# A list-scheduling planner that orders by due time instead of by rank, and six more tiles of exponents turned through DRAM, in a fused attention and state-space kernel

## The chip, the cores and the metric

The kernel runs on one core of a Trainium2 chip. The metric is the device time of one execution in microseconds, as the median of three runs. All arithmetic is float32, but for the mask and some idle matmuls.

## What is computed

The input is `X` of 4 batches x 1024 tokens x 256 features. Four residual layers follow one another, each on a layernorm of the running `x` (cut from the reference, with the names that the kernel uses in front):

```python
# a: causal attention
scores = where(causal, -inf, Q @ K.T / 16);  x = x + softmax(scores) @ V
# f: a feed-forward that mixes each token with the one before it
xr, xk = mu * xn + (1 - mu) * xn_prev
x = x + sigmoid(xr @ W_r.T) * (relu(xk @ W_k.T) ** 2 @ W_v.T)
# h, s: a state-space layer: projections, a causal convolution over the whole
#       sequence with 16 decay kernels, a skip and a gate silu(z)
x = x + (((conv(xp @ W_B.T) @ W_C.T + D_skip * xp) * silu(z)) @ W_out.T + b_out)
# g: the feed-forward once more, with the same weights
```

## The kernel before

**Tiles.** The whole `x` stays on chip. The tokens are cut into 32 tiles `i` of 128 (batch `i // 8`, place in the batch `t = i % 8`) and into 8 halves `j` of 512 (four tiles). Attention works by tiles: `scores(i)` (L1075) multiplies the queries of a tile with the `t + 1` blocks of keys before it; VectorE takes out the row extreme while it copies them to SBUF (`least`, L1098), ScalarE takes the exponents (`exponents`, L1108), the exponents are turned so that keys lie on partitions, and `weigh(i)` (L1181) multiplies them with the values (`po` on TensorE). The other layers work by halves.

**Two ways to turn.** `turn(i)` (L1158) has TensorE transpose each 128x128 block into PSUM (`ppt`), and ScalarE or VectorE copies it out. `turn_by_dram(i)` (L1124) has SyncE write the exponents to DRAM (L1135, `exps<-pr`), read them back in four pieces in another order (L1141, `pblocks<-exps`), and VectorE transposes 32x32 blocks (L1146, `prT<-pblocks`). Before the change the tiles with `t` of 0 and 1 of every batch take the first way and those with `t` of 2 to 7 the second (`TURNED_BY_DRAM = 2`, L38, used at L1100, L1490 and L1496). The normalized halves of layers a, f, h and g are turned through DRAM as well (`by_dram`, L482: one write of 512 KB at L489, four reads at L495, two transposes at L501), except four at the seams.

**The planner.** The order in which instructions stand on each engine is not written by hand but worked out when the kernel is built, by the class `Order` (L48). TensorE's work is a list of *units* in a fixed order, the order in which the main loop (L1486) and the lines behind it call them. All else is *ops*: a key, the keys it needs, one or more engines with a cost in us, and a lag until the result can be used. A unit first lets the planner place every op that can start by then (L121), and then takes TensorE for its own cost. Among the ops on offer the one with the earliest start goes first; of those with the same start (the engine is busy and several are waiting) the one with the lowest `rank`, then the one that was ready first (L94 to L96). Ranks: 0 for most; 1 for the normalizations of a, f and h on VectorE (L385); 2 for `by_dram`'s DMAs; 3 for loads, stores and the decay table (L247, L691, L806, L1339). Each engine then runs its list strictly in order, SyncE's DMA queue too, and waits in place for what an instruction needs.

**Hand-set holds.** `normalized` (L374) has a parameter `after`. With it the 512 KB write of a normalized half waits in the plan until the reads of a given tile of exponents have been issued and their lag has passed (`behind`, L995; given at L1010, L1221 and L1517).

**Loads.** `load` (L243) puts a planned time `at` on a list of transfers. Only the last transfer of a list carries the key that others need (L247). One list is `mu` (L311, at 14.0): two transfers for `muk` and then two for `mur`. The op `mu1` (L367) has VectorE work out `1 - mu` from all four (`complements`, L364).

The loop that calls the units of attention:

```python
for i in range(-2, NI):
    first, second = mix_units(i)
    if i + 2 < NI:
        scores(i + 2)
        if (i + 2) % NT >= TURNED_BY_DRAM:
            turn_by_dram(i + 2)
    for unit in first:
        unit()
    if 0 <= i + 1 < NI and (i + 1) % NT < TURNED_BY_DRAM:
        turn(i + 1)
```

## Time and profile before

| what | us |
|---|---|
| median of three runs (475.33 to 476.75) | 475.8 |
| the profiled execution | 476.57 |
| its span, first to last instruction | 474.8 |
| TensorE busy, share of the span | 99% |
| VectorE, ScalarE, GpSimd busy | 67%, 40%, 23% |
| DMA engines busy, mean of 16 | 50% |

The profile is of one execution. Its engines are PE (TensorE matmul), PEld (its weight load), DVE (VectorE), ACT (ScalarE), POOL (GpSimd) and SPq (the DMA queue of SyncE). `L1189` is a line of the kernel. A line of the timeline gives the start, the time from the first start to the last end of a run of like instructions, the engine, the line, the operation, what it writes and reads, and in brackets how long the engine was idle before it and what ended that. A matmul's recorded duration overlaps the next one's, so what a matmul costs is read from start to start.

### The profile page before, as it was taken

Reading aid. Unit: us, or ns where it says so; the run is one execution under the profiler, and the core shown is the slowest. Engines: PE = TensorE matmul, PEld = TensorE weight load, DVE = VectorE, ACT = ScalarE, POOL = GpSimd, SP = SyncE. Lnnn points to the kernel's source line nnn. Section 1 sums busy time; section 2 is a strip of 40 time slices with the busy share of each in tenths; the row PEclk is TensorE's granted clock in tenths of the full one; section 3 lists DMA queues with packets and bytes.
Section 4 is the critical chain, followed back from the end, with each engine's and each line's share of the span. In section 5 each row is a group of like instructions: output and inputs, shape, how many; then the busy total and the mean of one; then the engine's idle time right before and its main releaser. Section 6 shows DMA issues by size and latency. Waiting matters only on the chain.

```text
span 474.8 us, 6474 instructions
## 1 busy us (share of the span) xinstructions
PE 468.3 (99%) x2114; PEld 320.4 (67%) x2114; DVE 319.2 (67%) x856; ACT 190.2 (40%) x346; POOL 110.6 (23%) x119
## 2 busy tenths in 40 slices
PE   8999999999999999999999999999999999999996
PEld 5766676765866766866758766465565774877765
DVE  4657677698798797794986875410669794986312
ACT  3431435343346244344354385501113643535332
POOL 3020103101603304422223245300002210233330
PEclk9999999999999999999999999999999999999999
DMA  7649677634833944817249494902122706126112
GB/s 205 200 106 270 198 182 169 182 100 129 253 65 106 278 133 133 242 32 218 69 143 284 162 253 123 330 4 63 50 89 76 212 22 177 46 72 195 45 66 66
DMA packets 78289, 68.24 MB, mean 144 GB/s; under 512 B 13536, under 2 KB 75952, under 8 KB 78256
## 3 DMA queue, kind: packets, MB, share of 16 engines
q1 hardware_dynamic: 77440, 67.57, 48.9%
q8 instruction: 16, 0.26, 0.2%
q10 hardware_dynamic: 816, 0.26, 0.2%
q14 instruction: 17, 0.14, 0.1%
HBM read 39.95 MB, written 27.86 MB: 143 GB/s over the span
## 4 chain that ended last, share of the span: by engine, by line
PE 78%; DVE 10%; DMA 6%; SPq 3%; issue 2%; POOL 0%; ACT 0%; DVEq 0%; ACTq 0%
PE po L1189 8%; PE sc L1089 8%; PE py L1394 6%; PE pv L1061 3%; DMA pblocks<-exps 2%; DMA exps<-pr 2%; SPq L1141 2%; PE pc L1347 2%; DMA blocks_f<-rows_f 1%; PE dust L899 1%; DVE pr L1104 1%; DVE prT L1146 1%; PE py L1406 1%; SPq L495 1%; DVE hT_f L501 1%
## 5 line engine op out<-in xcount | busy, mean ns | idle before, releaser
L1189 PE MATMUL po<-v,prT 128*128 128x256 f32 x288 | 67.9, 380 | 0.5 <-DVE prT L1146 0.5
L1089 PE MATMUL sc<-xa,q 128*128 128x512 f32 (+3 forms) x192 | 67.2, 486 | 0.0
L1189 PEld LDWEIGHTS po<-v,prT 128*128 128x128 f32 x288 | 54.1, 189 | 11.0 <-issue 2.1
L1109 ACT ACTIVATE pr<-pr,nmx 128x128 f32<-128x128 f32 (+7 forms) x32 | 24.8, 774 | 71.9 <-DVE pr L1104 66.5
L1089 PEld LDWEIGHTS sc<-xa,q 128*128 128x128 f32 x192 | 35.1, 190 | 23.4 <-issue 18.9
L1061 PE MATMUL pv<-wv,xa 128*128 128x257 f32 x128 | 33.5, 384 | 0.0
L680 POOL TENSOR_TENSOR x<-x,r_f 128x512 f32<-128x512 f32 x16 | 22.5, 1410 | 40.0 <-DVE r_f L674 40.0
L427 POOL TENSOR_TENSOR rs_h<-ve_h,minus_half 128x8 f32<-128x8 f32 x8 | 13.2, 1646 | 78.1 <-DVE ve_f L414 38.9
L1104 DVE TENSOR_SCALAR_CACHE_REDUCE pr<-sc,v 128x128 f32<-128x128 f32 (+7 forms) x32 | 25.6, 799 | 7.0 <-PE sc L1096 6.8
L1146 DVE STREAM_TRANSPOSE prT<-pblocks 128x384 f32<-128x384 f32 (+5 forms) x24 | 21.7, 905 | 10.7 <-DMA pblocks<-exps 10.7
L1394 PE MATMUL py<-xnT,wk 128*128 128x512 f32 x64 | 28.8, 595 | 0.0
L1061 PEld LDWEIGHTS pv<-wv,xa 128*128 128x128 f32 x128 | 23.2, 191 | 8.0 <-issue 4.8
L680 POOL TENSOR_TENSOR x<-x,r_g 128x512 f32<-128x512 f32 x14 | 18.9, 1355 | 35.2 <-DVE r_g L674 34.2
L1234 POOL TENSOR_TENSOR x<-x,bout_r 128x512 f32<-128x512 f32 x16 | 20.2, 1274 | 26.8 <-ACT x L1227 17.7
L427 POOL TENSOR_TENSOR rs_g<-ve_g,minus_half 128x4 f32<-128x4 f32 x8 | 8.4, 1045 | 74.5 <-DVE ve_g L414 74.5
L1416 DVE SCALAR_TENSOR_TENSOR z<-py,b_skip,z 128x512 f32<-128x512 f32 x16 | 10.9, 743 | 21.6 <-PE py L1406 21.6
L1199 DVE SCALAR_TENSOR_TENSOR x<-po,rsm,x 128x256 f32<-128x256 f32 x32 | 15.5, 483 | 14.3 <-PE po L1189 11.2
L1394 PEld LDWEIGHTS py<-xnT,wk 128*128 128x128 f32 x64 | 12.0, 190 | 13.7 <-issue 13.5
L595 ACT ACTIVATE xk_g<-hT_g,muk 128x512 f32<-128x512 f32 x16 | 10.6, 712 | 20.3 <-DVE hT_g L501 20.3
L595 ACT ACTIVATE xk_f<-hT_f,muk 128x512 f32<-128x512 f32 x16 | 10.7, 714 | 19.7 <-DVE hT_f L501 11.8
L1227 ACT ACTIVATE x<-x,mrs_h,rs 128x256 f32<-128x256 f32 x32 | 17.5, 588 | 0.0
L1071 DVE TENSOR_TENSOR v<-pv,bv_r 128x257 f32<-128x257 f32 x32 | 13.2, 412 | 4.4 <-PE pv L1061 4.0
(431 smaller groups left out, 948.7 us busy)
## 6 DMA issues: line engine op xcount, KB each, us to landing
hk<-r_dram SPq DMA_DIRECT2D x16, 512.0 KB, 8.9
rows_g<-xn_g SPq DMA_DIRECT2D x8, 512.0 KB
blocks_g<-rows_g SPq DMA_DIRECT2D x32, 128.0 KB, 2.7
x<-in_L_attn_a_X_dram SPq DMA_DIRECT2D x7, 512.0 KB, 4.3
rows_f<-xn_f SPq DMA_DIRECT2D x7, 512.0 KB
blocks_f<-rows_f SPq DMA_DIRECT2D x28, 128.0 KB, 2.7
rows_h<-xn_h SPq DMA_DIRECT2D x7, 512.0 KB, 4.4
blocks_h<-rows_h SPq DMA_DIRECT2D x28, 128.0 KB, 3.0
```

Of the source, the lines that this page charges most:

```text
L427: nc.gpsimd.tensor_tensor(rs()[:, :k].rearrange("p k n -> p (k n)"), ve()[:, :k].rearrange("p k n -> p (k n)"), minus_half[:, : k * NH], A ...
L595: nc.scalar.mul(t()[:, c, :], hT()[:, c, 1:], mu[:, c : c + 1])
L680: nc.gpsimd.tensor_add(xg, xg, r()[:, ts(g, 2), :])
L1061: nc.tensor.matmul(pv()[:, : D + 1], lhsT=xaj()[:, c, ts(n, P)], rhs=wv[:, c, :], start=(c == 0), stop=(c == KC - 1),)
L1089: nc.tensor.matmul(sc()[:, k * HALF : k * HALF + w], lhsT=qh()[:, c, ts(n, P)], rhs=keys[k]()[:, c, :w], start=(c == 0), stop=(c == KC - 1 ...
L1104: nc.vector.tensor_scalar(dst, src, vh()[:, n, D : D + 1], None, ALU.add, ALU.min, accum_out=nmx(),)
L1109: nc.scalar.activation(p()[:, :nk], p()[:, :nk], AF.Exp, bias=nmx(), scale=-1.0, accum_out=sm())
L1146: nc.vector.transpose(dst()[:, : NH * width].rearrange("p (k m a) -> p k m a", m=NH, a=GRP), blocks().rearrange("p m (k a) -> p k m a", a= ...
L1189: nc.tensor.matmul(po()[:, :D], lhsT=src()[:, ts(n, P)], rhs=v[2 * b + n // NH]()[:, n % NH, :D], start=(n == 0), stop=(n == t),)
L1227: nc.scalar.activation(xt, xt, AF.Identity, bias=mrs()[:, 0, n : n + 1], scale=rs1()[:, n : n + 1])
L1234: nc.gpsimd.tensor_add(xg, xg, bout_r.unsqueeze(1).to_broadcast([P, 2, D]))
L1394: nc.tensor.matmul(dst()[:, ts(e, HALF)], lhsT=w_x[:, c, ts(e, P)], rhs=src()[:, c, :], start=(c == 0), stop=False,)
```

## The change

The class `Order` first writes everything into a log, and places it only in `finish`. In between it works out a due time for each entry, backwards. Ranks and `after` are gone; `behind` is deleted. `TURNED_BY_DRAM` keeps its value of 2 and is now compared with the tile's number instead of its place in the batch, so that only tiles 0 and 1 are turned by TensorE, and tiles 8, 9, 16, 17, 24 and 25 go through DRAM. What `op`, `unit` and `_step` did with the engines' times stays as it was.

```diff
+    def op(self, key, needs, *ways, frees=None, delay=0.0, lag=LAG):
+        self.log.append(dict(
+            kind="op", key=key, needs=needs, ways=ways, frees=frees, delay=delay, lag=lag,
+            cost=min(c for _, c, _ in ways),
+        ))
...
+    def _due(self):
+        log = self.log
+        made = {e["key"]: n for n, e in enumerate(log) if e["key"] is not None}
+        due = [math.inf] * len(log)
+        at = 0.0
+        takes = {kind: [] for kind in self.BANKS}
+        for n, e in enumerate(log):
+            if e["kind"] == "unit":
+                due[n] = at
+                at += e["cost"]
+            if e.get("takes"):
+                takes[e["takes"]].append(at)
+        given = {kind: 0 for kind in self.BANKS}
+        for n, e in enumerate(log):
+            if e["kind"] == "op" and e["frees"]:
+                kind = e["frees"]
+                k = given[kind] + self.BANKS[kind]
+                given[kind] += 1
+                if k < len(takes[kind]):
+                    due[n] = takes[kind][k] - self.LAG - e["cost"]
+        order = self._sorted(made)
+        for n in reversed(order):
+            e = log[n]
+            for k in e["needs"]:
+                m = made[k]
+                if log[m]["kind"] in ("op", "unit"):
+                    d = due[n] - e.get("delay", 0.0) - log[m]["lag"] - log[m]["cost"]
+                    due[m] = min(due[m], d)
+        return due
...
     def _first(self):
-        start, _, _, n = min(
-            (self._way(op)[1], op["rank"], op["time"], n) for n, op in enumerate(self.offered)
+        start, _, _, k = min(
+            (self._way(time, n)[1], self.due[n], time, k)
+            for k, (time, n) in enumerate(self.offered)
         )
...
-            o.op(key if last else None, [f"t{at}", *after], (queue, 0.5, emit), lag=lag, rank=3)
+            o.op(key if last else None, [f"t{at}", *after], (queue, 0.5, emit), lag=lag)
...
-            by_dram(key, xn, parts + list(after), dst, names)
+            by_dram(key, xn, parts, dst, names)
...
-    def behind(i):
-        if not 0 <= i < NB * NT:
-            return []
-        return [f"e{i}.r{P // GRP - 1}" if i % NT >= TURNED_BY_DRAM else f"e{i}"]
...
-            if t >= TURNED_BY_DRAM:
+            if i >= TURNED_BY_DRAM:
...
-            if (i + 2) % NT >= TURNED_BY_DRAM:
+            if i + 2 >= TURNED_BY_DRAM:
                 turn_by_dram(i + 2)
...
-        if 0 <= i + 1 < NI and (i + 1) % NT < TURNED_BY_DRAM:
+        if 0 <= i + 1 < TURNED_BY_DRAM:
             turn(i + 1)
...
-                mix1.prepare(i // NH, by_hand=i == NI - 1, after=behind(i + 3 if i < 27 else 29))
+                mix1.prepare(i // NH, by_hand=i == NI - 1)
```

An op whose key is `None`, or whose result nothing further needs, keeps a due time of infinity, unless it frees a PSUM bank.

## Prediction

> **What bounds the kernel now.** I read the page first, then TensorE's own waits, then its timeline by starts, and last the queues that feed it. The page's busy shares:

> ```profile
> PE 468.3 (99%) x2114; PEld 320.4 (67%) x2114; DVE 319.2 (67%) x856; ACT 190.2 (40%) x346; POOL 110.6 (23%) x119
> PE 78%; DVE 10%; DMA 6%; SPq 3%; issue 2%; POOL 0%; ACT 0%; DVEq 0%; ACTq 0%
> ```

> The chain (second line) gives other engines 22%, but it follows releasers, and an engine that keeps TensorE just fed counts too. The waits of TensorE itself are three, all short:

> ```profile
> PE dust L899 <- DVE idle L235: 1.2, 1, 1.2
> PE pp_f2.pk L541 <- DVE xk_f L598: 0.8, 1, 0.8
> PE po L1189 <- DVE prT L1146: 0.5, 1, 0.5
> ```

> So TensorE's instruction stream is the bound nearly throughout, and only work taken out of it, or waits taken out of or put into it, move the time. The floor is close: the start and the tail are not touched, and what can go is worked out below as 2.7 us. What can come has no such limit.

> **Nine transposes go.** TensorE's timeline shows one place of each size:

> ```profile
> 63.01 0.28 PE L1168 MATMUL ppt<-ident,pr 128*128 128x128 f32 x1
> 63.13 1.03 PE L1061 MATMUL pv<-wv,xa 128*128 128x257 f32 x4
> 139.41 0.38 PE L1168 MATMUL ppt<-ident,pr 128*128 128x128 f32 x2
> 139.63 1.03 PE L1061 MATMUL pv<-wv,xa 128*128 128x257 f32 x4
> ```

> From start to next start they cost 0.12 and 0.22 us. Batches 1, 2 and 3 each lose one of each: 3 x 0.34 = **-1.0 us**, all of it on the bound. [...] The rows say 0.11 us each in a full stream, and the sum keeps that.

> **What takes their place.** Six times one write and four reads on SP: 6 x (0.38 + 1.73) = 12.7 us of issue by the rows of 192 KB tiles. Their landings: 2.3 us for the write and 1.8 for the reads (192 KB tile, the smallest), 3.9 and 3.0 at most (512 KB). Six VectorE transposes of 128 or 256 columns: by the 574 ns at 384 and the 1239 ns at 1024 about 0.31 and 0.44 us, 2.2 us in all, against six copies of 0.24 to 0.42 us that go. The write of the extremes in another order costs nothing visible: 353, 480, 606 and 725 ns at 128, 256, 384 and 512 columns is one straight line across both layouts. Tile 8's scores end at 58.1 and its `po` starts at 73.44; extremes, exponents, write, reads and transpose are about 8 to 11 us by these rows. Some 4 us are left, more for tile 9. I take **0**. If that cover were gone, each late tile would cost its lateness. [...]

> **Two waits of TensorE.** The wait at 136.6 us:

> ```profile
> 136.53 0.22 PE L1096 MATMUL sc<-mask,ident_b 128*128 128x128 bf16 x1
> 137.59 1.98 PE L541 MATMUL pp_f2.pk<-xk_f,w_fk 128*128 128x512 f32 x4 [0.84 <-DVE xk_f L598]
> 105.81 0.42 DVE L410 BATCH_NORM_STATS2 st_h<-x 128x6 f32<-128x256 f32 x1
> 110.15 0.42 DVE L410 BATCH_NORM_STATS2 st_f<-x 128x6 f32<-128x256 f32 x1
> 123.48 0.44 SPq L489 DMA_DIRECT2D rows_f<-xn_f  x1
> ```

> A mask matmul steps on after 0.05 us elsewhere; here it takes 1.06, so 1.0 is lost. Half f2's rows were complete at 97.5 (tile 11's `po`), but half h0, which TensorE first reads at 272, had its statistics in front, and the write waited for the hold on tile 14 and two other writes. By due time f2 stands near 137 less a dozen us, h0 near 260: f2 goes first. Next late is the gate's `xr_f`, already in time. **-1.0**.

> The other: `pv` starts at 43.35 and `po` of tile 4 at 44.94, 1.59 against 0.87, so 0.72 is lost. Its reads (issued 37.73 to 39.62) landed at 43.9, behind `rows_a` (36.20) and a load of `x` (36.74), 512 KB each. `rows_a` was ready at 28.75 and held by `after`; freed, it goes out some 7 us earlier, leaving one transfer in front. **-0.7**, less sure.

> **One wait that I expect to come.** In `load` only the last transfer of a list has a key; the others now have no due time and lose every tie. For `mu` (planned at 14.0) the second `mur` goes first and `mu1` is thought ready at 14.0 + 0.5 + 3.0 = 17.5 instead of 19.0. The real first `mur` goes last, behind a 512 KB load of `x` and `w_fv`. Today:

> ```profile
> 17.51 1.11 SPq L104 DMA_DIRECT2D mur<-in_L_ffn_mu_r_dram  x2
> 18.66 0.47 SPq L104 DMA_DIRECT2D x<-in_L_attn_a_X_dram  x1
> 19.17 0.51 SPq L104 DMA_DIRECT2D w_fv<-in_L_ffn_W_v_dram  x1
> ...
> 19.04 0.48 DVE L1104 TENSOR_SCALAR_CACHE_REDUCE pr<-sc,v 128x256 f32<-128x256 f32 x1 [0.49 <-PE sc L1096]
> 20.20 0.17 DVE L364 TENSOR_SCALAR mur<-mur 128x2 f32<-128x2 f32 x1 [0.67 <-DMA mur<-in_L_ffn_mu_r_dram]
> 21.17 0.39 PE L1168 MATMUL ppt<-ident,pr 128*128 128x128 f32 x2
> ```

> VectorE idles 0.49 us just before the extremes of tile 1 (19.04); planned 1.5 us earlier, `mu1` falls into that gap and stands in front of them. The same issue times in the new order (`mur`, `x`, two `muk`, `w_fv`, `mur`, from 16.13) put the last issue's end near 19.75. Today `mu1` starts 1.58 us after it: 21.3. Add 0.3 for `mu1`, 1.03 from the start of the extremes to the end of the exponents (19.04 to 20.07), 0.1 to start: tile 1's transpose, still on TensorE, starts at 22.75 instead of 21.17. Queued behind `mu1` are tile 1's extremes, the values and the extremes of tile 2; TensorE waits for the first. **+1.5**. Ends: 0 if `mu1` stays behind the extremes; +3.4 if the last `mur` lands 4.6 us after `w_fv` is issued, as `w_fv` itself does today (19.17 to 23.79).

> **The holds gone otherwise, and order by due time on VectorE, ScalarE and GpSimd.** The trace shows none of it. Ends: -0.5 (the waits of 0.1 us at a dozen unit starts) to +4 (third rival). I take **0**: between 152 and 470 us TensorE loses no single wait above 0.11 us, so that stretch has cover.

> **Sum.** -1.0 - 1.0 - 0.7 + 1.5 = -1.2. Span 474.8 becomes 473.6; with the 1.8 us outside it the profiled execution's 476.6 becomes 475.4. That execution lies 0.8 above the median of 475.8, so the median becomes **474.6**, which counts as no change: 0.3% (1.4 us: 474.4 to 477.2) is about what a measurement of this kernel can tell.

> **Rivals.**
> *`mu1` does no harm.* For it: VectorE's gap is half a microsecond, and a planned start later by 0.7 puts `mu1` behind the extremes. Against: that gap is in the plan too, since VectorE waits there for TensorE. Without the +1.5: **473.1**, faster.
> *512 KB writes get in front of exponents: slower.* Place: batch 0, 28 to 64 us, where a tile takes only 4 to 7 us:

> ```profile
> 55.30 1.25 SPq L489 DMA_DIRECT2D rows_f<-xn_f  x1
> 62.57 1.25 DVE L1146 STREAM_TRANSPOSE prT<-pblocks 128x1024 f32<-128x1024 f32 x1 [2.88 <-DMA pblocks<-exps]
> 64.00 3.62 PE L1189 MATMUL po<-v,prT 128*128 128x256 f32 x16
> ```

> Tile 7's turn ends at 63.82, 0.2 before its `po`. Its write was issued at 54.82; `rows_f` and the next `rows_a` follow at 55.30 and 61.95, held. Both in front are 1.05 MB, 3.0 us at the 351 GB/s of 57 to 58 us: 2.8 us of wait. It decides once a write stands in front of a tile with less slack than its own 1.5 us. Against: half f0 could go out near 46. 474.6 + 2.8 = **477.4**; at a second tile, 480.
> *The change does little.* List order is set by the earliest start first, and due time only breaks ties; f2 and tile 4 stay late. -1.0 + 1.5 gives **476.3**.

> **Chances.** Forecast (473.9 to 475.6) 0.40, first rival 0.25, second 0.25, third 0.10. Faster: 0.25 + 0.12 of the forecast's lower edge + 0.01 = 0.38; slower: 0.20 of the second rival + 0.02 = 0.22; same 0.40. Range: 472.6 (all gains, no `mu1`, some small waits gone) to 478.4 (one tile late and `mu1` at 2.5), which leaves some 2 in 10 outside.

> **What would show it.** `ppt` x3 instead of x12; no wait at `pp_f2.pk`, `st_f` of f2 before `st_h` of h0, `rows_f` for it near 105 to 110; `rows_a` near 29 to 30 and no wait at tile 4's `po`; the order of `mur`, `x`, `muk`, `w_fv` on SP, VectorE waiting for `mur` at 18.5 to 21.3 in front of tile 1's extremes, and TensorE waiting at its second `ppt`. New waits of `po` for `prT` before 66 us are the second rival. I am wrong altogether if a new wait above 0.5 us stands after 152 us.

## The result, and the profile after

The changed kernel takes 483.28 us in the median of four runs (482.62 to 484.6), the kernel before 476.0 us in four runs beside them: a ratio of 1.0156, 95% interval 1.0129 to 1.0183. It is 1.6% **slower**, 7.3 us, and lies above the predicted range (472.6 to 478.4). The profiled execution took 482.62 us with a span of 480.8 us, 6.0 us more than before.

From the page after: the busy shares, the granted clock in 40 slices of 12 us, and the chain by engine.

```profile
PE 471.4 (98%) x2105; PEld 321.2 (67%) x2105; DVE 322.0 (67%) x850; ACT 195.0 (41%) x353; POOL 108.0 (22%) x118
PEclk9899989999999999999999999999999999999999
PE 80%; DMA 9%; DVE 5%; SPq 3%; issue 1%; ACT 1%; DVEq 0%; ACTq 0%
```

TensorE has nine instructions fewer (2105 against 2114) and is busy 3.1 us longer. The second line says how: slices 2 and 6, 12 to 24 us and 60 to 72 us, stand at 8 tenths of full clock. TensorE's own waits after (instruction, what it waited for, us in total, times, longest):

```profile
PE po L1251 <- DVE rsm L1260: 2.6, 1, 2.6
...
PE pt_a0.xa L1084 <- DVE xn_a L513: 0.7, 1, 0.7
PE pw_bx L933 <- DVE x L1261: 0.7, 1, 0.7
```

The waits at `pp_f2.pk` and at tile 4's `po` are gone, as forecast. Three new ones stand there: at the start (`pt_a0`), at tile 7 (`po`) and at 202 us (`pw_bx`).

The waits alone come to 4 us and the loss to 6. To see the rest, take one instruction of TensorE's fixed order in both timelines and subtract the starts: where this offset steps, time is lost or won. The first `after` row of the table below gives, step by step: 2.82 us lost by the first `pv`; 0.67 won at tile 4; 2.77 lost at tile 7's `po` and 1.51 more by the first `pp_f0.pk`; 0.39 won up to the 19th `pv`, most of it the transposes of tiles 9 and 16 that are gone (0.22 and 0.12); 0.95 won at `pp_f2.pk` and 0.27 just behind it; 1.20 lost by `pw_bx`, 0.3 of it at a `po` at 194.4 us. Hardly anything moves after 203 us.

**The start.** The first rows of `x` now leave behind `wk` (1.23 us instead of 0.74), VectorE starts their statistics at 5.72 instead of 4.24 and then stands in front of the product `wq` (L1032) with the second `xn_a` queued behind it. TensorE waits 0.73 us in the middle of its transposes, and three microseconds later this is its stretch (us, busy time of PE, PEld, DVE, ACT and POOL, granted clock, DMA share, GB/s), first after, then before:

```profile
14.00:16.00 2.00, 2.00 (x3) 0.67 (x2) 1.80 (x8) 0.00 (x0) 0.00 (x0) 0.50 0.24 55
```

```profile
14.00:16.00 2.00, 2.00 (x7) 1.02 (x6) 0.81 (x5) 0.86 (x2) 1.01 (x1) 1.00 0.68 156
```

Both call TensorE fully busy; after, it starts 3 matmuls in the time of 7. The eight matmuls of `pq` take 5.24 us instead of 3.53. Of the 2.82 us, 1.36 are there by `pb_w` (11.30 against 9.94); 0.25 of them are caught up before `pq`, and the slow clock costs 1.71, so 1.46 net.

**Tile 7.** SyncE's queue after, from the turn of tile 6 on (start, issue time, transfers):

```profile
52.20 0.38 SPq L1197 DMA_DIRECT2D exps<-pr  x1
52.68 0.45 SPq L559 DMA_DIRECT2D rows_f<-xn_f  x1
55.18 2.52 SPq L1203 DMA_DIRECT2D pblocks<-exps  x4
57.87 1.73 SPq L565 DMA_DIRECT2D blocks_f<-rows_f  x4
59.70 0.38 SPq L1197 DMA_DIRECT2D exps<-pr  x1
60.19 0.44 SPq L559 DMA_DIRECT2D rows_a<-xn_a  x1
63.23 1.75 SPq L1203 DMA_DIRECT2D pblocks<-exps  x4
```

The exponents of tile 7 are complete at 58.48 (ScalarE). Their write goes out at 59.70, behind the four reads of `f0`, whose product `pp_f0.pk` starts only at 75.25. Before, the order was tile 7's write, `f0`'s write, tile 7's reads, `f0`'s reads. Further up the same chain, the write of tile 4 (37.67) stands behind a load of `x` and four reads of `a2`, that of tile 5 behind the other load of `x`. The chain of waits gives what the writes of tiles 4, 5 and 7 then take to land (before, tile 4's took 2.55; tile 5's, issued at 40.61 with its reads at 45.72, was already as slow):

```profile
37.67 5.00 DMA exps<-pr
...
45.06 5.25 DMA exps<-pr
...
59.70 3.48 DMA exps<-pr
```

VectorE stands still meanwhile and reads tile 7's extremes at 55.95 instead of 51.70. At the end of it:

```profile
65.23 1.09 PE L1123 MATMUL pv<-wv,xa 128*128 128x257 f32 x4
68.92 5.14 PE L1251 MATMUL po<-v,prT 128*128 128x256 f32 x16 [2.60 <-DVE rsm L1260]
```

That `po` took 3.62 us before. Its 5.14 are the clock again, 0.50 at 69 to 71 us.

**`pw_bx`.** The bank that it needs is freed by VectorE's residual addition at 202.35, which is queued behind tile 23's turn:

```profile
200.95 1.25 DVE L1208 STREAM_TRANSPOSE prT<-pblocks 128x1024 f32<-128x1024 f32 x1 [2.12 <-DMA pblocks<-exps]
202.35 0.48 DVE L1261 SCALAR_TENSOR_TENSOR x<-po,rsm,x 128x256 f32<-128x256 f32 x1
```

That turn is late from two sides. VectorE reads the extremes of tile 23 at 188.50, 2.6 us after its scores, because the normalization of an h half, a layer whose turn comes at 278 us, stands in front (three `xn_h` from 186.01, then tile 22's turn). And the exponents, complete at 190.93, are written at 192.42, behind four reads of `a7` (189.68) and two of that h half (191.53). This is read from the two queues; no run repairs this place alone.

### The profile page after: what moved, and what is told of

The parts are those of the page before. It is cut to its first block, busy times and chain, and to the rows that moved or that the text cites. A ratio compares the mean times of both kernels' runs of the same rounds, so it can differ in the third digit from the quotient of the medians.

```text
span 480.8 us, 6508 instructions
## 1 busy us (share of the span) xinstructions
PE 471.4 (98%) x2105; PEld 321.2 (67%) x2105; DVE 322.0 (67%) x850; ACT 195.0 (41%) x353; POOL 108.0 (22%) x118
## 4 chain that ended last, share of the span: by engine, by line
PE 80%; DMA 9%; DVE 5%; SPq 3%; issue 1%; ACT 1%; DVEq 0%; ACTq 0%
PE po L1251 9%; PE sc L1151 8%; PE py L1455 6%; DMA exps<-pr 5%; PE pv L1123 4%; SPq L1203 2%; DMA pblocks<-exps 2%; PE pc L1408 1%; PE pp_a0.pq L611 1%; DVE pr L1166 1%; PE py L1467 1%; DMA wq<-in_L_attn_a_Wq_dram 1%; DVE prT L1208 1%; PE pb L1350 1%; PE pr_g1.pv L626 1%
## 5 line engine op out<-in xcount | busy, mean ns | idle before, releaser
L1251 PE MATMUL po<-v,prT 128*128 128x256 f32 x288 | 69.5, 386 | 2.7 <-DVE rsm L1260 2.6
L749 POOL TENSOR_TENSOR x<-x,r_f 128x512 f32<-128x512 f32 x16 | 20.3, 1271 | 70.2 <-DVE r_f L743 54.4
L1208 DVE STREAM_TRANSPOSE prT<-pblocks 128x384 f32<-128x384 f32 (+7 forms) x30 | 24.0, 799 | 14.1 <-DMA pblocks<-exps 14.0
L498 POOL TENSOR_TENSOR rs_g<-ve_g,minus_half 128x4 f32<-128x4 f32 x8 | 9.4, 1178 | 72.4 <-DVE ve_g L485 72.3
L498 POOL TENSOR_TENSOR rs_f<-ve_f,minus_half 128x4 f32<-128x4 f32 x8 | 8.1, 1013 | 72.9 <-DVE ve_f L485 59.9
L498 POOL TENSOR_TENSOR rs_h<-ve_h,minus_half 128x8 f32<-128x8 f32 x8 | 13.2, 1648 | 19.1 <-DVE ve_h L487 17.5
```

Source lines behind the costliest of these rows:

```text
L498: nc.gpsimd.tensor_tensor(rs()[:, :k].rearrange("p k n -> p (k n)"), ve()[:, :k].rearrange("p k n -> p (k n)"), minus_half[:, : k * NH], A ...
L749: nc.gpsimd.tensor_add(xg, xg, r()[:, ts(g, 2), :])
L1208: nc.vector.transpose(dst()[:, : NH * width].rearrange("p (k m a) -> p k m a", m=NH, a=GRP), blocks().rearrange("p m (k a) -> p k m a", a= ...
L1251: nc.tensor.matmul(po()[:, :D], lhsT=src()[:, ts(n, P)], rhs=v[2 * b + n // NH]()[:, n % NH, :D], start=(n == 0), stop=(n == t),)
```

## The experiments

The **theory** after the result: the due order does what it says (f2, tile 4), and loses at a few places where a transfer or an op that is not due for long starts a little earlier in the plan than one that is due, and then stands in front of it in an engine's strict order; two of these waits take TensorE's clock down (to 0.50), which adds 1.5 us to each. **Rivals**: the late start pushes all the rest; the missing holds alone are to blame; the six tiles through DRAM are to blame.

All 18 kernels stand in one table (`b_rank` with two series). "Median" and the ratio are those of the timed runs (the kernel before had medians of 476.0 to 477.55 beside them); the other columns belong to the one profiled execution and give the offset of TensorE's start, in us, against the kernel before, at: the first `pv` (15.62 us there), the transposes of `a1` just behind tile 1's `ppt` (21.39), tile 4's `po` (44.94), tile 7's `po` (64.00), the first `pp_f0.pk` (68.82), the 19th `pv` (130.91), `pp_f2.pk` (137.59), `pw_bx` (196.86), the 27th `pv` (202.26); and the span's difference. The start differs from run to run (with the order of the kernel before, `pv1` lies between -0.90 and 0.50; the two idle matmuls in front of the first transpose of `wk` step on after 0.43 us each in `before`, after 0.215 in `b_rank_again`), so the steps between columns are to be read. A profiled run need not be a typical one: that of `a_turnpe` is the lowest of its seven (478.71), that of `a_start` the highest of its four. For `a_dust` the first true matmul of `po` is taken.

```
kernel             median ratio   pv1   a1    po4   po7   f0    pv19  f2    pw_bx pv27  span
after              483.28 1.0156  2.82  2.82  2.15  4.92  6.43  6.04  5.09  6.03  6.02   6.0
a_start            486.07 1.0179 -0.10  1.54  0.92  4.21  5.69  5.30  4.35  9.78 13.12  13.1
a_start_mu         484.08 1.0134  0.18  0.18 -0.12  1.81  1.90  2.06  1.12  7.40  7.40   7.4
a_dust0            483.37 1.0128  0.33  1.78  1.11  3.93  4.02  3.64  2.69  6.19  6.18   6.2
a_dust             483.10 1.0136  2.12  2.12  1.46  4.15  4.14  3.75  2.80  4.39  6.06   6.1
a_holds            479.28 1.0036  0.12  1.63  0.97  3.20  3.29  2.91  1.96  2.64  2.53   2.3
a_mu_holds         478.90 1.0047  0.36  0.36  0.49  2.56  2.66  2.27  1.33  2.01  2.58   2.4
a_mu_holds_f0      480.16 1.0073 -0.62 -0.62 -0.77  0.37  0.77  0.44 -0.51  1.19  1.83   1.6
a_mu_holds_f0_lx   483.36 1.0125 -0.02 -0.02 -0.68 -0.84 -0.86  2.60  1.71  6.76  6.64   6.4
a_turnpe           481.41 1.0090  2.01  2.01  1.35  2.59  2.68  2.63  1.63  1.58  1.58   1.8
a_mu_pe            477.23 1.0016 -0.69 -0.69  0.37  2.20  2.29  2.24  1.24  1.92  2.03   2.3
a_mu_holds_f0_pe   479.78 1.0070  0.23  0.23 -0.44  1.10  1.19  1.19  0.76  2.71  2.71   2.9
a_mu_f0_pe_lx      480.83 1.0076 -0.75 -0.75 -1.06 -0.92  0.41  4.53  3.53  3.68  3.78   4.0
b_turn             482.70 1.0108 -0.74 -0.75  0.77  0.71  0.73  0.85 -0.10  6.34  6.23   6.0
b_rank             477.07 1.0018 -0.48 -0.48 -1.15 -1.25 -1.26 -1.31 -2.32 -2.37 -2.37  -2.0
b_rank_again       476.49 1.0016 -0.90 -0.89  1.48  4.45  4.43  4.39  3.38  3.33  3.33   3.6
b_rank_turn        479.07 1.0054 -0.79 -0.79 -1.05 -1.11 -0.74 -0.61 -1.56 -1.12  2.18   2.2
b_lx               474.75 0.9966  0.50  0.50 -0.16 -0.26 -0.28 -0.33 -1.33 -1.17 -1.17  -1.2
b_rank_lx          476.11 0.9997 -0.25 -0.25 -0.92 -1.02 -1.03 -1.08 -2.09 -1.69 -1.39  -0.8
```

### The start and `mu1`

`a_start` puts `x` ahead of `wk` again:

```diff
-    load(0.0, "wk", *natural_rows(wk, WkT, nc.sync), lag=4.3)
+    load(0.4, "wk", *natural_rows(wk, WkT, nc.sync), lag=4.3)
```

> The changed kernel with one number changed: `wk` is planned at 0.4 instead of 0.0 us, so that SyncE issues the first rows of x ahead of it, as in the kernel before. Theory (loss of the start = order of the first loads, made larger by the clock): the first pv, at 18.44 us in the changed kernel and 15.62 before, comes back to 15.6 to 16.0, and no row of the clock below 0.9 stands at 12 to 18 us. What is gained by that meets the second theory at tile 1: `mu1` then stands in front of tile 1's extremes while TensorE is not late, so TensorE waits 1 to 2 us at its second ppt, and of the 2.8 us only 0.9 to 1.8 are left: about 481.5 to 482.4 in the median (changed kernel 483.3). If `mu1` is harmless, 2.8 us are left: 480.5. Rival for tile 7 (the start's lateness is what pushed the exponents behind the loads of x): tile 7's wait, 2.6 us, goes too and the time falls below 479. Rival for the start (the clock fell by itself): pv stays near 18.4 and the time near 483.

The start's loss is gone (`pv1` -0.10), and at once `mu1` costs what was forecast, a step of 1.64 us:

```profile
21.03 0.47 DVE L436 TENSOR_SCALAR mur<-mur 128x2 f32<-128x2 f32 x1 [2.59 <-DMA mur<-in_L_ffn_mu_r_dram]
...
21.49 0.47 DVE L1166 TENSOR_SCALAR_CACHE_REDUCE pr<-sc,v 128x256 f32<-128x256 f32 x1
```

```profile
22.66 0.44 PE L1230 MATMUL ppt<-ident,pr 128*128 128x128 f32 x2 [1.42 <-ACT pr L1171]
```

VectorE waits for the last `mur` with tile 1's extremes (21.49) behind it, and TensorE's second `ppt` starts at 22.66 (forecast: 22.75). Tile 7 still loses 3.29 us and 1.48 to the clock (0.50 from 67.6 us on) with a start that is not late, so the rival of the late start falls. The median did not come down: in the profiled run, the highest of four (483.68 to 489.79), TensorE waits 0.7 and 1.6 us at 155 and 182 us for `r_f` and `ka_f`, and then `pw_bx` waits 2.6 us and loses the clock too (0.50 from 207.6 to 214.4 us; 9.78 to 13.12). That a gain early turns into a loss later is the pattern of nearly all that follows.

`a_start_mu` is `a_start`, and gives the other transfers of a load list the due time of the keyed one (`like` is that one's key):

```diff
+        for n, e in enumerate(log):
+            if e.get("like"):
+                due[n] = due[made[e["like"]]]
```

> As a_start, and every transfer of a list of loads gets the due time of the list's last one, which alone has a key, so that the first `mur` is no longer issued last. Theory (`mu1` in front of tile 1's extremes costs TensorE 1 to 2 us as soon as TensorE is not late anyway): the second ppt starts near 21.2 us, as in the kernel before, against about 22.3 to 23 in a_start; the time is 1 to 2 us below a_start's, about 480.5. Rival (`mu1` was harmless): same time as a_start, same second ppt. In both theories tile 7 keeps its wait of 2 to 3 us for its exponents, because nothing is changed there; if it goes, the lateness of the start was its cause.

The step at `a1` is 0.00: `mu1`'s cost is shown, and shown to come from the load without a due time. Tile 7 loses 1.93 us and nothing to the clock. The time, 484.08, is above the 480.5 expected: 6.3 us go between f2 and `pw_bx`, in waits of TensorE for `r_f` (1.7) and `ka_f` (1.5, and 1.7 by the clock of 0.50 behind it), which the changed kernel does not have, and at `pw_bx` itself (1.1).

`a_dust0` fills the wait at the start with eight idle matmuls and changes nothing else:

```diff
+                        if j == 0 and c == 0 and n == 1:
+                            for _ in range(8):
+                                nc.tensor.matmul(
+                                    pt[c]()[:, D:], lhsT=idle[:, :P], rhs=idle[:, :D],
+                                    start=True, stop=True,
+                                )
```

> The changed kernel with eight idle matmuls of 256 columns (bf16, about 0.11 us each) on TensorE between the first two transposes of half a0, where it waits 0.73 us; they write columns that the later transposes overwrite. Theory (of the 2.8 us at the start, 1.5 are the clock, which falls for a few us behind that wait): the first pv is late by 1.0 to 1.6 instead of 2.8, its eight pq matmuls take 3.5 us instead of 5.2, and no 2 us stretch from 10 to 20 us has a clock below 0.9. Tile 7 loses as before. The time falls by up to 1.5 us, less if the next transfers are late anyway. Rival (the clock falls there for another reason, such as the first loads): 14 to 16 us stays near 0.50 and pv late by 2.8.

```profile
14.00:16.00 2.00, 2.00 (x6) 0.80 (x5) 1.05 (x5) 0.69 (x1) 0.76 (x1) 1.00 0.32 88
```

The clock holds, `pq` takes 3.53 us, and from `pb_w` to `pv1` 0.24 us are won instead of 1.46 lost: the wait was the cause. The other runs agree: the mean clock of the four is 0.996 to 1.0, that of the changed kernel's four 0.992 to 0.995. In its place comes `mu1`, 1.45 us. A wait of 0.52 us at the same spot (`a_holds`) left the clock at 1.00; one of 0.73 (`a_dust`, `a_turnpe`) was followed by a clock of 0.50 from 12.56 and 12.52 us on, for 3.4 us.

### Tile 7

`a_dust` puts 26 idle matmuls in front of tile 7's `po`:

```diff
+            if i == 7:
+                for _ in range(26):
+                    nc.tensor.matmul(
+                        po()[:, :D], lhsT=idle[:, :P], rhs=idle[:, :D], start=True, stop=True
+                    )
```

> The changed kernel with 26 idle matmuls of 256 columns (bf16) added on TensorE in front of tile 7's po, into the bank that po overwrites; they wait for nothing, and the planner knows nothing of them. At about 0.11 us each they fill 2.8 us, the gap in front of that po. Theory (1.5 of the 4.4 us lost at tile 7 are the clock, which falls because TensorE stood still): tile 7's po still starts late, by 4.9 us against the kernel before, but its 16 matmuls take 3.5 us instead of 5.0, the clock stays above 0.9 at 68 to 72 us, and f0's first matmul is late by 4.9 instead of 6.4: 1.5 us below the changed kernel, about 481.8. Rival (the clock falls for another reason, or the matmuls behind the gap are slow for their data): no row changes and the time is 483.3 or, with the added work, more.

```profile
65.31 3.00 PE L1252 MATMUL po<-idle 128*128 128x256 bf16 x26
68.15 3.63 PE L1256 MATMUL po<-v,prT 128*128 128x256 f32 x16
```

`po` is as late as in the changed kernel (2.69 us after tile 4's offset, there 2.77), and what follows it costs nothing more, as against 1.51 us of slow clock in the changed kernel. That the filling kept the clock up is not shown, though: `a_dust0`, without it, kept its clock at 1.00 through a wait of 2.81 us at the same place (last section). The total is the changed kernel's all the same, because `pw_bx` now waits 1.4 us, and the clock is at 0.50 from 203.7 us on:

```profile
201.25 1.08 PE L933 MATMUL pw_bx<-w_b,w_xt 128*128 128x32 f32 x8 [1.44 <-DVE x L1266]
...
202.61 4.96 PE L1256 MATMUL po<-v,prT 128*128 128x256 f32 x14
```

`a_holds` puts the hand-set holds back (`after=behind(...)` at its three places).

> The changed kernel with the hand-set holds put back: the normalized rows' way through DRAM waits again for the named tile's exponents. The due order, the order of the first loads and the two tiles on TensorE stay as changed. Theory (loss at tile 7 = the holds gone, so that f0's and a1's reads and writes stand in front of e5, e6, e7 on SyncE): the wait of 2.6 us at tile 7's po goes and with it the slow clock behind it, 4.4 us, while f2 keeps its early place only if its hold no longer matters: about 479, or 480 if f2 waits again. Rival (the due order puts loads of x and f0's reads ahead of the exponents whether held or not): the wait at tile 7 stays within 0.5 us of 2.6 and the time within 1 us of 483.3. Rival (the late start is the cause): the same.

The time is as expected and the reason is not. Tile 7 still waits 2.2 us: on SyncE `f0`'s write and two of its reads stand in front of tile 7's, hold or no hold, since `f0`'s hold is on tile 6. `pw_bx` does not wait here; in its place the `po` of tile 17 waits 0.69 us for `r_f` at 154.8 us, a step of 0.95. The rest of the difference is a clock that stays up at tile 7 in the profiled run (six of the ten runs have 0.995 or 0.996), and a start that is 2.7 us earlier: about 0.9 of it is there when the wait at the start ends (10.0 us against 10.91), the rest comes with the clock that then stays up, less 1.5 for `mu1`. That start is no work of the holds. So the missing holds explain a part, and not tile 7.

`a_mu_holds` is `a_start_mu` with the holds.

> All three repairs at once on the changed kernel: x's first rows ahead of `wk`, the due time of a list's last load given to the others, and the hand-set holds back. Theory (the terms add up): of the held kernel's 479.3 the wait for mu1 goes, 1.5 us, while tile 7's wait of about 2 us stays, because f0's write and two of its reads still stand in front of tile 7's write and reads on SyncE: about 477.5 to 478, no wait of TensorE at its second ppt, one of 1.5 to 2.2 at tile 7's po, none above 0.5 us at pw_bx. Rival (tile 7 is late because everything before it is late): its wait falls below 0.7 us and the time to 476 or less.

Steps as forecast: no wait at the second `ppt`, tile 7 2.07, none at `pw_bx` itself; but two `po`, at 154 and 201 us, wait 0.69 and 0.52 us for `r_f`. The median, 478.9, is 0.9 above the band.

`a_mu_holds_f0` adds an order for `f0` by hand:

```diff
-        o.op(f"{key}.w", needs, ("SP", 0.45, write), lag=2.2)
+        tile7 = key == "f0"
+        o.op(f"{key}.w", needs + ["e7"] * tile7, ("SP", 0.45, write), lag=2.2)
...
-            o.op(f"{key}.r{j}", [f"{key}.w"], ("SP", 0.45, partial(read, j)), lag=late)
+            o.op(
+                f"{key}.r{j}", [f"{key}.w"] + ["e7.w"] * tile7,
+                ("SP", 0.45, partial(read, j)), lag=late, delay=1.9 * tile7,
+            )
```

> As the kernel with three repairs, and one more: f0's write waits in the plan for tile 7's exponents and f0's reads for tile 7's write and 1.9 us, which puts them on SyncE in the order of the kernel before (tile 7's write, f0's write, tile 7's reads, f0's reads). The due order stays for all the rest. Theory (what stands in front of tile 7's exponents on SyncE is the loss there): the wait at tile 7's po falls from about 2 us to 0.5 or less, f0's first matmul waits for nothing, and the time falls by 1.5 to 2 us, to 475.5 to 476: at or just below the kernel before, since the gains at f2 (1.0) and of nine transposes (1.0) are then no longer covered. Rival (something earlier, such as the loads of x in front of tiles 4 to 6, makes tile 7 late): the wait stays above 1.3 us and the time does not move; or f0 is late now and its first pp waits 1 us or more.

Between the two theories: tile 7's loss halves, 2.07 to 1.14. `a_mu_holds_f0_lx` moves the last batch's loads of `x` as well:

```diff
-        load((14.0, 18.0, 34.0, 39.0)[j - 4], f"xl{1 + j}", *tokens(b, h * NH, (h + 1) * NH))
+        load((14.0, 18.0, 70.0, 75.0)[j - 4], f"xl{1 + j}", *tokens(b, h * NH, (h + 1) * NH))
```

> As the kernel with three repairs and f0's transfers behind tile 7's, and the last batch's two loads of x planned at 70 and 75 us instead of 34 and 39. Theory (512 KB of x in front of tile 4's and tile 5's exponents made their turn late by 2 us, and through VectorE tile 7's extremes): the wait at tile 7's po falls from 1.0 us to below 0.4, and TensorE's offset against the kernel before at 69 us is at most that of its start. Rival (the bursts do not matter, the rest comes from where VectorE does the extremes): the wait stays at 0.8 or more.

The rest is gone: a step of -0.16 at tile 7. Its cause is thus shown and has two halves, `f0`'s transfers and 512 KB of `x` in front of exponents. Yet the kernel is no faster than the changed one. Its waits of TensorE:

```profile
PE po L1267 <- DVE ka_f L713: 1.9, 1, 1.9
PE po L1267 <- DVE q L1124: 1.2, 1, 1.2
...
PE pv L1139 <- DVE r_f L754: 1.0, 1, 1.0
PE pd L864 <- ACT q L1122: 0.6, 1, 0.6
```

Each is a PSUM bank that an op on VectorE or ScalarE has yet to empty. The second, on VectorE:

```profile
119.46 0.42 DVE L487 BATCH_NORM_STATS2 st_h<-x 128x6 f32<-128x256 f32 x1
119.91 0.18 DVE L488 BATCH_NORM_AGGREGATE mv_h<-st_h 128x2 f32<-128x6 f32 x1
120.01 0.72 DVE L1124 TENSOR_SCALAR q<-pp_a4.pq,bm 128x512 f32<-128x512 f32 x1
```

`pq` ended on TensorE at about 115.4; the op that empties it starts at 120.01, behind four statistics of a half of h, the layer that is due last. By the code, the op with the earliest planned start goes first and due time decides only between equals; that the plan had the statistics start first is concluded from the order, not tried. Nor is a second point of the code: `_due` notes a unit's taking of a bank after it has added the unit's cost, so an op that frees a bank is due later by that cost, for a `pq` some 3.5 us.

### Exponents through DRAM

`b_turn` makes this part of the change alone, in the kernel before (`i` for `t` at the places that compare with `TURNED_BY_DRAM`):

> The kernel before with one part of the change: only tiles 0 and 1 of the first batch keep their exponents' turn on TensorE, six more tiles go through DRAM; rank order and holds stay. Theory (nine transposes leave the bound, what replaces them is hidden): ppt x3, TensorE's starts at 152 us earlier by 0.3 and at the end by 1.0, 474.8 to 475.2 in the median (before 476.0). [...]

Slower by 1.08% (interval 0.78 to 1.39), 5.1 us. TensorE's waits:

```profile
PE pp_f3.pk L541 <- DVE xk_f L598: 3.6, 1, 3.6
PE po L1189 <- DVE prT L1146: 2.0, 1, 2.0
```

The second is at tile 4, at 45.7 us, ahead of tile 8's scores and all that the change touches, and so belongs to the kernel before. The first is the change. On SyncE:

```profile
155.45 0.38 SPq L489 DMA_DIRECT2D rows_a<-xn_a  x1
155.93 0.44 SPq L489 DMA_DIRECT2D rows_f<-xn_f  x1
157.02 0.36 SPq L1135 DMA_DIRECT2D exps<-pr  x1
159.41 1.78 SPq L495 DMA_DIRECT2D blocks_a<-rows_a  x4
161.28 0.85 SPq L495 DMA_DIRECT2D blocks_f<-rows_f  x2
162.18 2.05 SPq L1141 DMA_DIRECT2D pblocks<-exps  x4
164.27 0.91 SPq L495 DMA_DIRECT2D blocks_f<-rows_f  x2
```

`f3`'s write leaves 3.1 us later than before (152.84), behind `a6`'s, and its last reads 5 us later. No small tile stands there: the added ops moved the plan, and the two halves changed places. With the clock (0.50 at 172 to 178 us) the wait of 3.6 us costs 6.7.

`a_turnpe` undoes this part alone, in the changed kernel.

> The changed kernel with the other half undone: tiles 8, 9, 16, 17, 24 and 25 turn their exponents on TensorE again (12 transposes of tiles as before), the planner stays as changed. Theory (nine transposes are worth 0.11 us each on the bound, what replaces them is hidden): ppt x12, 1.0 us more than the changed kernel, about 484.3, with the same losses at the start and at tile 7. Rival (the six small tiles' writes and reads delay others on SyncE, as they seem to do under the old order at f3): a later stage gains more than 1.0, and the time is 483 or less.

481.41 us, 1.9 below the changed kernel and not 1.0 above. In the profiled run, the lowest of seven, tile 7's wait is shorter (a step of 1.24, and no clock lost), and `pw_bx` does not wait: the plan has moved, the h half is normalized elsewhere, and tile 23's extremes are read 1.3 us after its scores instead of 2.6.

`b_rank_turn` repeats `b_turn` on a kernel in which the h halves rank behind f3 (`b_rank`, below).

> As the kernel with the later rank, and tiles 8, 9, 16, 17, 24, 25 turned through DRAM. Theory A (the nine transposes are worth 1.0 us, and the loss of 6 us in the first try was one accident at f3, where a half that was not due went in front of f3's reads): the wait at pp_f3.pk goes with the rank, and the time is 1.0 us below the one without the turn, 2.0 below the kernel before. Theory B (six more writes and 24 more reads on SyncE delay something each time, whatever the order): a wait of TensorE above 0.5 us appears somewhere after 66 us, and the time is above that of the kernel without the turn.

f3 is in time; at 198 us a `po` waits 1.6 us for `r_f` instead, with the clock behind it (0.50 from 199.1 to 202.5 us): the median is 2.0 us above that of `b_rank`. Theory B, then, though not by the small transfers themselves. The five pairs that differ in these six tiles alone:

| pair (TensorE, DRAM) | ratios | DRAM costs, us |
|---|---|---|
| before, `b_turn` | 1, 1.0108 | 5.1 |
| `b_rank`, `b_rank_turn` | 1.0018, 1.0054 | 1.7 |
| `a_turnpe`, after | 1.0090, 1.0156 | 3.1 |
| `a_mu_pe`, `a_start_mu` | 1.0016, 1.0134 | 5.6 |
| `a_mu_holds_f0_pe`, `a_mu_holds_f0` | 1.0070, 1.0073 | 0.1 |

(Each difference times 476.) TensorE does win its 0.34 us a batch, seen in the steps of `after` at the 19th `pv` and behind `pp_f2.pk` (0.12 and 0.22); in no pair is it left at the end.

### The due order with TensorE's tiles

`a_mu_pe` is `a_start_mu` with these tiles on TensorE, `a_mu_holds_f0_pe` is `a_mu_holds_f0` with them, and `a_mu_f0_pe_lx` has start, `mu`, `f0` and the loads of `x` repaired, without holds.

> The changed kernel's due order without holds, with x's first rows ahead of `wk` and `mu`'s transfers due together, and with tiles 8, 9, 16, 17, 24, 25 on TensorE. The terms measured so far: start 2.0 and clock behind it gone, mu1 absent, tile 4 0.3 to 0.7 gained, tile 7 1.2 lost, f2 1.0 gained, nothing lost at pw_bx: TensorE's offset against the kernel before at 200 us is -0.7 to 0, the time that of the kernel before within 0.7 us. Rival (each repair moves the plan, and the due order makes a new wait elsewhere as in the earlier two repairs): an offset above 1.0 us with a wait at a place not seen before, 478 or more.

> All repairs: due order, x ahead of `wk`, `mu` due together, holds back, f0's transfers behind tile 7's, and tiles 8, 9, 16, 17, 24, 25 on TensorE. In batch 0 SyncE's order is then that of the kernel before. Theory (what the due order lost came from these places alone): nothing lost up to 70 us, f2's 1.0 gained, about 1.0 us below the kernel before. Rival (the due order puts statistics of halves that are not due in front of ka_f on VectorE, as at 173 to 176 us in the kernel with f0 behind tile 7): TensorE waits 1.6 us at f3's ka_f or another such place, and the time is 0.5 to 2 above the kernel before.

> Due order without holds, start and `mu` repaired, f0 behind tile 7, loads of x late, tiles 8, 9, 16, 17, 24, 25 on TensorE. Theory (all that the due order lost was found): no wait of TensorE above 0.7 us after 5 us, f2's 1.0 and tile 4's 0.7 gained: 475 to 476, 0.5 to 1.5 below the kernel before. Rival (f0 is late now, since a2's reads stand among its own on SyncE; or a new wait elsewhere): a wait of 1 us or more at pp_f0.pk or later, 477 or more.

The first is the best of the due order, 1.0016 (0.9998 to 1.0034): no gain, with 1.08 us lost at tile 4 and 1.82 at tile 7. Against 1.0156 of the changed kernel, the start, `mu` and the six tiles together give back 6.7 us of the 7.3. Beyond that, the more is repaired, the slower: in the second TensorE waits 0.9 us at tile 7 and 0.7 and 0.8 us at 142 and 145 us, in the third 1.1 us at `pp_f0.pk` and 2.2 us at a `po` at 129.6 us. Both times the rival.

### A version that beats both

`b_rank` changes one rank in the kernel before (h one half step lower, its DMAs too):

```diff
-        rank = 0 if key[0] == "g" else 1
+        rank = {"g": 0, "f": 1, "a": 1, "h": 1.5}[key[0]]
```

> The kernel before with one number changed: the normalization in front of the state-space layer (halves h0 to h7) ranks half a step behind the other two, on every engine and on SyncE. Old planner, holds, and eight tiles on TensorE stay. Theory (the 1.0 us at f2.pk is lost because h0's statistics and transfers, not needed for 130 us, stand in front of f2's): the wait of 0.8 us at pp_f2.pk goes, nothing else moves, 1.0 us less than the kernel before. Rival (the hold on tile 14 sets f2's write, not h0): the wait stays and the time is the same. Rival (what is gained there is lost at the next half f3, where h0's reads now come late): a wait at f3 of 0.5 us or more.

> The kernel with h ranked later, once more. Theory (f2's 1.0 us is real and the first series was blurred by runs at a lower clock): median 1.0 us below the kernel before. Rival: the median is that of the kernel before again, and then the wait at f2 was not on the path of most runs.

The wait at f2 goes in both profiles (steps of -1.01 and -1.06), no other comes, and neither median falls: 1.0018 (0.9995 to 1.0040) and 1.0016 (0.9991 to 1.0041). Where the 1.0 us went in the runs without a profile is not shown; in each series three of the twelve runs have a mean clock of 0.993 to 0.996, at 478.6 to 480.2 us. The second series' profile is of such a run, 480.21 us at 0.993. It shows:

```profile
46.42 4.63 PE L1189 MATMUL po<-v,prT 128*128 128x256 f32 x10 [2.88 <-DVE prT L1146]
```

```profile
48.00:50.00 2.00, 2.00 (x6) 1.55 (x5) 1.03 (x7) 0.65 (x2) 1.03 (x2) 0.50 0.95 272
```

Tile 4's wait, 0.49 us in the profile of before, is 2.88 us here with the same instructions in front, and the clock costs 2.96 us on top.

`b_lx` takes the two loads of `x` away from tile 4 in the kernel before (the diff of `_lx` above, nothing else); `b_rank_lx` has both.

> The kernel before with the last batch's two loads of x planned at 70 and 75 us instead of 34 and 39. Theory (512 KB of x in front of tile 4's reads on SyncE make the wait at tile 4's po, 0.5 us in one run and 2 in another with the same instructions, and that wait sometimes takes the clock down): no wait of TensorE at tile 4's po, 0.7 us less in the median, and hardly a run at a clock of 0.996. Rival (the bursts do not matter there; the clock falls elsewhere): same median, as many runs 3 us higher.

> Both: h ranked later and the loads of x late. Theory: the gains add up, no wait of TensorE after the first 2 us, 1.7 us less than the kernel before in the median (0.4%), which would be the fastest of all. Rival: what is not waited for here is waited for later (loads of x at 70 us in front of tile 10 and the Mamba weights), and the median stays within 0.5 us.

`b_lx` takes **474.75 us** (473.94 to 475.55) against 476.19 beside it: 0.9966 (0.9945 to 0.9988), faster than both kernels, in one series. Tile 4 no longer waits, and since the plan moved, f2 does not either (a step of -1.00). None of its twelve runs has a mean clock below 0.999; of the 29 runs of the kernel before beside it four have 0.995 or 0.996, at 478.1 to 479.9 us. `b_rank_lx` adds nothing: 0.9997, with a wait of 0.3 us at `pw_bx`.

## Why the prediction was wrong

**The bound.** The prediction's "the start and the tail are not touched" is the first step that failed: the start lost 2.82 us. The queue's order at 0.7 us (`x`, `wk`, `x`) was in the trace, and the due order changes it as it changes all else. 1.36 us are the later landing (`wq` is taken up at 5.03 us instead of 4.67, the first rows of `x` at 5.72 instead of 4.24) and the order on VectorE, 1.46 net the clock.

**Nine transposes, -1.0.** 0.12 and 0.22 a batch, 1.0 in all. Right. (Of its rows for the extremes, the 353 and 480 ns are 351 and 478 in batch 0; nothing hangs on it.)

**What takes their place, 0.** Wrong. Slack was counted for the small tiles' own `po` (some 4 us), and no `po` of theirs waited for its exponents; what was late were others, f3 in one plan, tiles 7 and 23 in the other. In the changed kernel the six tiles cost 3.1 us net by the ratios (1.9 by the medians), after their own gain.

**Two waits, -1.0 and -0.7.** Measured -0.95 and -0.67. The first has the reason given: `st_f` of f2 now stands before `st_h` (104.36 and 116.68), and `b_rank`, which only ranks h later, loses the wait too. The second is luck as far as the runs show: TensorE is 2.8 us late at tile 4 in the changed kernel, and with the start repaired 0.30 us are won there in `a_start_mu` and 1.08 lost in `a_mu_pe`.

**`mu1`, +1.5.** The mechanism, the order on SyncE and the size were right (1.64, 1.45 and 1.51 us where the start is not late) and the sum was wrong: in the changed kernel TensorE is already 2.8 us late there, and `mu1` costs 0.00. A wait is paid only where no earlier one has covered it.

**Holds and due order elsewhere, 0.** This is the term that decided. "Between ends far apart" (-0.5 to +4) the middle was taken, because TensorE has cover from 152 to 470 us; but the loss is at tile 7, 2.77 us and 1.51 by the clock, and 1.20 at `pw_bx`. The second rival named the place, the slack of 0.2 us and 2.8 us of wait for it. Its transfers were only partly those named: not 512 KB writes but `f0`'s four reads, and loads of `x` that no hold had ever touched. It got 0.25 and is what happened. The holds, which were the suspects, do not prevent it at tile 7; they do at `pw_bx`.

**The clock.** No term of the sum had it. Of the 6.0 us, some 3 are matmuls at half clock behind two waits. The page of before has full clock in every slice, so it gave no sign of this price.

**"Wrong altogether if a new wait above 0.5 us stands after 152 us."** It stands at `pw_bx`, 0.73 us.

## What to carry to other kernels

In these plans, as far as the queues show, a due time that only breaks ties does not keep an undue op out of a strict queue: the planner starts what can start, and what is due a microsecond later waits behind it; so read in each queue what stands just in front of the op that TensorE needs next. Where TensorE is the bound, a wait had three prices here: its length (2.81 us in `a_dust0`), its length and some 1.5 us or more of slow clock (2.60 and 1.51 in the changed kernel; the length alone does not tell which, next section), or nothing where TensorE was already late (`mu1` in the changed kernel, 0.00). Repairs to a global order do not add up: the kernel in which the start, `mu`, the holds and tile 7 were all repaired (`a_mu_holds_f0_lx`) takes what the unrepaired one takes, while one pair of loads moved in the old order (`b_lx`) gained more than all of them.

## What the runs showed of the hardware

**The length of a wait alone did not tell whether the clock fell.** In the 20 profiles, of TensorE's waits of 1.4 to 3.7 us behind the first 5 us, ten were followed by a clock of 0.50 for 3.4 or 6.8 us (1.44, 1.52, 1.57, 1.92, 2.17, 2.55, 2.60, 2.85, 2.88 and 3.62 us) and twelve by a full one (1.42, 1.56, 1.57, 1.59, 1.60, 1.66, 1.66, 1.82, 1.97, 2.01, 2.23 and 2.81). Of the shorter ones, from 0.45 us on, only that of 0.73 us at the start did it, in all three profiles that have it. The longest that cost nothing, in `a_dust0` at tile 7, the matmul and then two stretches (clock third from the end):

```profile
67.93 3.73 PE L1257 MATMUL po<-v,prT 128*128 128x256 f32 x16 [2.81 <-DVE rsm L1266]
```

```profile
66.00:68.00 2.00, 0.07 (x1) 0.07 (x1) 1.29 (x2) 0.00 (x0) 0.00 (x0) 1.00 0.92 192
68.00:70.00 2.00, 2.00 (x10) 1.76 (x11) 1.98 (x6) 0.60 (x2) 0.00 (x0) 1.00 0.08 12
```

What parts the falls from the rest, where the timelines allow a count, is how long TensorE streams columns in a step. From start to start 512 columns take 0.43 us in float32 and 0.215 in bf16 (`before`, the bf16 ones at 6.90 to 7.55 us), so 0.84 and 0.42 ns a column; a matmul of one column steps on after 0.11 us, and so counts for almost nothing. Counted like this, the two falls of `after` end steps with 1.26 us (at 13.80) and 1.09 us (at 68.42) of streaming, and none of the 266 other steps at full clock in `before` and `after` has less than 1.29 (the one that ends at 204.95 us in `after`, with the wait at `pw_bx` in it). In three more profiles the falls at 45.6 (`b_rank_again`), 130.8 (`a_mu_f0_pe_lx`) and 180.3 us (`a_mu_holds_f0_lx`) end steps with about 1.1, 1.2 and 0.1, and no other step at full clock has less than 1.6. So a wait of 0.73 us at the start, 0.52 of it in the step, was enough: twelve one-column matmuls (`pb_w`) stand in the same step. This was found in the traces afterwards and not tried on a new run, and the two limits are close.

**A write landed late behind other transfers.** The write of tile 4's exponents took 2.55 us with only small loads issued in the two microseconds before it (35.11 us, kernel before), and 5.00 us behind four reads and a load of `x`, 512 KB each in total, issued in the three microseconds before it (37.67 us, changed kernel); that of tile 5 took 5.25 us there, 0.5 us behind the other load of `x`.
